# A fused group norm and attention kernel: TensorE keeps the kernel's own order, sums follow one burst later, and a batch's output projection runs beside the load two pairs further on

## The chip, the core and the metric

The kernel runs on one core of a Trainium2 chip. Five engines work side by side, each through its own queue of instructions: TensorE (PE, matrix products; its weight loads are shown as PEld), VectorE (DVE), ScalarE (ACT), GpSimd (POOL) and SyncE (SP). SP only issues DMA transfers here. The other engines can issue DMAs too, and DMA engines move the data. Instructions of different engines wait for each other through semaphores. [...]

The metric is the device time of one execution in microseconds (us), the median of several runs. The profile comes from one further execution, recorded by the hardware profiler.

## What is computed

The input x has 4 batches of 512 channels by 48 x 48 = 2304 positions. It is normalized in 32 groups of 16 channels, goes through attention with 8 heads of 64 channels, is projected, and is added to x again:

```python
hn = _group_norm(x, gn_scale, gn_bias)                # 32 groups, fp32
qkv = jnp.einsum('oc,bchw->bohw', qkv_w, hn) + qkv_b[None, :, None, None]
qkv = qkv.reshape(b, 3, num_heads, d, t).astype(jnp.float16)
q, k, v = (qkv[:, 0], qkv[:, 1], qkv[:, 2])
scale = jnp.asarray(1.0 / math.sqrt(math.sqrt(d)), dtype=jnp.float16)
w = jnp.einsum('bhct,bhcs->bhts', q * scale, k * scale)
w = jax.nn.softmax(w, axis=-1)
a = jnp.einsum('bhts,bhcs->bhct', w, v).astype(jnp.float32)
out = jnp.einsum('oc,bchw->bohw', proj_w, a.reshape(b, c, hh, ww)) + proj_b[None, :, None, None]
return x + out
```

## The kernel before

**Tiles and stages.** Channels lie on the 128 partitions, so a batch of x is four chunks of 128 x 2304. Two heads together fill 128 channels. The kernel therefore works on 16 pairs of heads in order, g = 4 x batch + pair. The queries of a pair are cut into five blocks (`QBLOCKS`): four of 512 and one of 256.

The work of a pair is cut into units. A unit covers 512 query columns in all: one key block of 128 keys for the blocks of 512 queries, two key blocks for the block of 256. That makes 4 x 18 + 9 = 81 units in a pair (`units_of`, L735). For a unit:

- `scores` (L743) computes keys times queries for both heads (L751) into a PSUM tile `ps` of 128 x 1024; there are two such tiles. One exp on ACT (L759) turns it into a tile `p` in fp16; there are six. No maximum is subtracted. DVE adds the p tiles of up to six units into a tile `acc` (L772).
- `values` (L774) multiplies v with p and sums over all keys of a block into a PSUM tile `av` (L787); there is one such tile. After six units a matmul with ones sums the columns of `acc` into the PSUM tile `sl` (L801).
- `finish` (L811), after the last keys of a block, copies `av` to `avx` (L815) and `sl` to `slx` (L817) on DVE, sends the sums through SP's DMAs and DRAM (`sums`, the reciprocal `inv`, `row`, then `ib`, the sums spread over the partitions), and multiplies `avx` by `ib` on POOL into the attention output `att` (L833).

Units go in bursts of two: the scores of a burst, then the values of the burst before, then `fill` (L883). The pair has an odd number of units, so in every second pair a burst holds the last unit of one block and the first of the next.

**Work beside the bursts.** What else PE must do is cut into items, kept in a list per pair (`beside`, filled by `put`, L843). Each item has a weight in us, and can have a place, a unit of the pair before which it isn't taken. `fill` takes items from the head of the list until their weights have caught up with the share of the pair's units that are done; an item whose place has not come stops the list. When the scores of pair g + 1 begin, what is left of pair g's list is run at once.

The items are:

- `qk_items(g)` (L614): q and k of pair g from the normalized x, in fp32. For each of five column blocks and four chunks of channels an item has two matmuls of 64 output rows (L629). After the fourth chunk DVE moves the result to fp16 with scale and bias (L638).
- `v_items(b)` (L663): v of a whole batch, 18 blocks of 128 positions by four chunks (L673), two matmuls of 64 output rows each; DVE adds the bias (L681).
- `proj_items(b, j)` (L693): the output projection for one query block. POOL casts `att` of four pairs to a tile `a32` (L700), of which there is one. Then come four row blocks m of eight matmuls each (L710: the projection weights are split into a high and a low part, `whi` and `wlo`), written as items of one channel chunk each. For each m SP loads a tile of x again, `res` (three buffers), DVE adds projection, bias and x (L719), and SP stores it.
- `turn` (L850): `load_x` for the next batch (L497, two DMAs for each chunk on POOL's queue, into the single buffers of x), then `norm` (L572): statistics on DVE (L577), means over groups by two small matmuls on PE (`gmean` L580, `gvar` L590), a power on POOL for 1/sqrt, and then four instructions of 128 x 2304 on DVE, one for each chunk, which apply the norm in place (L602).

All three kinds of items, and the small matmuls of the norm, use the same two PSUM tiles `pw`.

**Order.** The lists are filled in L848 to L869. For batches 0 to 2, pair 0 of a batch has q and k of pair 2 beside it, pair 1 those of pair 3, pair 2 has `turn` and the first 55 entries of the next batch's v, and pair 3 the rest of v, and q and k of the next batch's first pair (and of its second, but for batch 2). The projection of the batch before stands beside pairs 0 (four blocks) and 1 (one block). In the last batch each of the first three pairs has q and k of the next one; the last batch's own projection stands beside the last pair, each block's items not before 12 units after the block's end.

This is the order in which the instructions are written. [...] the built order of PE differs from the written one: in before the items' matmuls often stand between single units, and pieces of an item are apart.

**Start.** x of batch 0 is loaded over SP's and ACT's queues, the constants follow on SP's queue and the three parts of the q, k, v weights on ACT's. After the norm come q and k of pair 0, the splitting of the projection weights (`split_wproj`, L536: DMAs on SP, copies on DVE), v of batch 0, and q and k of pair 1. After the last burst the rest of the last projection runs as a tail, and a count over all sums sets a flag for a general path (`general_path`), which does not run with these inputs.

## Time and profile before

| what | us |
|---|---|
| median of 3 runs | 1922.71 (1918.26 to 1926.49) |
| profiled execution | 1919.6 |
| its span, first to last instruction | 1917.7 |

The busy time of each engine over the stretches of the profile that the first and last exp of a batch set (us; batch 0 holds pairs 0 to 3, and so on):

| stretch | length | PE | DVE | ACT | POOL |
|---|---|---|---|---|---|
| start, to the first exp | 160.1 | 127.6 | 49.1 | 1.3 | 3.1 |
| batch 0 | 446.1 | 426.2 | 268.4 | 315.0 | 31.7 |
| batch 1 | 453.5 | 441.0 | 281.7 | 314.2 | 45.2 |
| batch 2 | 427.5 | 412.7 | 276.7 | 314.2 | 44.4 |
| batch 3 | 402.4 | 393.6 | 256.5 | 314.5 | 46.0 |
| tail | 28.1 | 15.3 | 8.9 | 0.0 | 4.2 |

In the lines of a profile, L751 is line 751 of the kernel, "out<-in" names the tiles that an instruction writes and reads, then come partitions x elements of both, and "x4" how many instructions a line stands for. A bracket at the end of a line of the timeline names how long the engine stood idle before it, and what released it. "PEclk" and "clock" are the granted clock of PE as a share of full speed. [...]

### The profile page before, as it was taken

The page shows a single profiled execution, that of the slowest core. Times are in us where ns is not written, and L with a number is a line of the kernel's source. Part 1 is how long each engine was busy: PE and PEld are TensorE (multiplying, and loading weights), DVE is VectorE, ACT ScalarE, POOL GpSimd, SP SyncE. Part 2 cuts the span into 40 slices and gives each one's busy share as a digit, 9 for nine tenths or more (in the row PEclk, how much of TensorE's full clock was granted, in tenths as well). Part 3 has the DMA queues.
Part 4 walks back from the last instruction along what each step waited for, and adds up shares of the span by engine and source line. Part 5 has one row for each costly group of instructions (what it writes and reads, how often), then busy time and mean ns, then how long its engine had stood idle before and what let it go on. Part 6 is the DMA issues. An engine that isn't in the chain of part 4 may idle for free.

```text
span 1917.7 us, 27997 instructions
## 1 busy us (share of the span) xinstructions
PE 1816.3 (95%) x10644; PEld 656.0 (34%) x10644; DVE 1141.3 (60%) x1800; ACT 1259.2 (66%) x1297; POOL 174.7 (9%) x199
## 2 busy tenths in 40 slices
PE   3999999799999999989999999979999999999997
PEld 1333233223333353322333344332333344332334
DVE  5224566675555666685555566677566566665664
ACT  0005788685666768876665767877577767887872
POOL 0000000100000021110000011020000011000011
PEclk9999999899999999989999999989999999999998
DMA  5000000300000041310000032040000032010033
GB/s 203 1 1 1 12 15 18 108 12 12 9 7 14 23 144 34 121 34 12 9 12 7 15 99 90 13 143 12 12 9 12 15 107 82 18 46 12 15 100 104
DMA packets 88643, 82.20 MB, mean 43 GB/s; under 512 B 51636, under 2 KB 57780, under 8 KB 88500
## 3 DMA queue, kind: packets, MB, share of 16 engines
q1 hardware_dynamic: 82884, 60.67, 11.7%
q0 software_dynamic: 3456, 14.16, 2.0%
q10 hardware_dynamic: 2160, 5.51, 0.8%
q8 instruction: 85, 1.39, 0.3%
q14 instruction: 58, 0.48, 0.1%
HBM read 60.83 MB, written 19.17 MB: 42 GB/s over the span
## 4 chain that ended last, share of the span: by engine, by line
PE 78%; DMA 6%; ACT 5%; DVE 5%; issue 4%; POOL 1%; SPq 0%; ACTq 0%; DVEq 0%; POOLq 0%
PE pqk L629 26%; PE ps L751 16%; PE av L787 15%; PE pv L673 12%; PE pr L710 7%; ACT p L759 5%; PE sl L801 3%; DVE acc L772 3%; DMA x<-x_dram 2%; DMA out_dram<-x 1%; DMA sums<-slx 1%; DMA row<-inv 1%; DVE st L577 1%; DMA wqkv<-qkv_wT_dram 1%; DMA ib<-row 1%
## 5 line engine op out<-in xcount | busy, mean ns | idle before, releaser
L759 ACT ACTIVATE p<-ps 128x1024 f16<-128x1024 f32 x1296 | 1257.9, 1022 | 612.7 <-PE ps L751 583.5
L772 DVE TENSOR_TENSOR acc<-acc,p 128x1024 f16<-128x1024 f16 x848 | 617.3, 729 | 318.8 <-ACT p L759 305.8
L629 PE MATMUL pqk<-x,wqkv 128*64 128x512 f32 (+1 forms) x2560 | 621.4, 552 | 3.9 <-DVE x L602 3.9
L787 PE MATMUL av<-p,v 128*64 128x512 f16 (+1 forms) x2880 | 464.3, 374 | 2.2 <-DVE avx L815 2.2
L751 PE MATMUL ps<-q,k 64*128 64x512 f16 (+1 forms) x2880 | 448.1, 364 | 14.2 <-ACT p L759 7.1
L751 PEld LDWEIGHTS <-k 64*128 64x128 f16 x2880 | 120.7, 94 | 544.3 <-issue 534.4
L673 PE MATMUL pv<-wqkv,x 128*64 128x512 f32 x1152 | 278.3, 593 | 0.0
L629 PEld LDWEIGHTS pqk<-x,wqkv 128*64 128x64 f32 x2560 | 198.7, 137 | 190.1 <-issue 109.6
L772 DVE TENSOR_TENSOR acc<-p,p 128x1024 f16<-128x1024 f16 x224 | 157.2, 702 | 165.1 <-ACT p L759 163.9
L833 POOL TENSOR_TENSOR att<-avx,ib 128x512 f16<-128x512 f32 (+1 forms) x80 | 100.5, 1257 | 1537.0 <-DMA ib<-row 1302.1
L787 PEld LDWEIGHTS <-v 128*64 128x64 f16 x2880 | 128.9, 108 | 247.7 <-issue 241.8
L710 PE MATMUL pr<-a,whi 128*128 128x512 f32 (+1 forms) x320 | 131.5, 417 | 8.2 <-POOL a L700 6.1
L673 PEld LDWEIGHTS pv<-wqkv,x 128*64 128x64 f32 x1152 | 84.8, 137 | 114.6 <-issue 94.1
L710 PE MATMUL pr<-a,wlo 128*128 128x512 f32 (+1 forms) x320 | 121.5, 385 | 0.0
L801 PE MATMUL sl<-acc,ones 128*64 128x512 f16 (+1 forms) x512 | 95.7, 362 | 21.4 <-DVE acc L772 20.9
L681 DVE TENSOR_TENSOR v<-pv,bv 128x512 f16<-128x512 f32 x72 | 49.6, 689 | 71.5 <-PE pv L673 71.5
L815 DVE COPY avx<-av 128x512 f32<-128x512 f32 (+1 forms) x80 | 51.0, 637 | 55.6 <-PE av L787 55.5
L710 PEld LDWEIGHTS pr<-a,whi 128*128 128x128 f32 x320 | 61.4, 192 | 54.9 <-issue 24.6
L638 DVE TENSOR_SCALAR k<-pqk,bqk 128x512 f16<-128x512 f32 (+1 forms) x80 | 55.4, 692 | 35.2 <-PE pqk L629 34.7
L638 DVE TENSOR_SCALAR q<-pqk,bqk 128x512 f16<-128x512 f32 (+1 forms) x80 | 55.3, 691 | 35.3 <-PE pqk L629 34.3
L719 DVE SCALAR_TENSOR_TENSOR x<-pr,bproj,x 128x512 f32<-128x512 f32 (+1 forms) x80 | 55.3, 694 | 35.0 <-PE pr L710 22.6
L700 POOL CAST a<-att 128x512 fp32r<-128x512 f16 (+1 forms) x80 | 53.9, 705 | 143.7 <-PE pr L710 142.8
(41 smaller groups left out, 281.2 us busy)
## 6 DMA issues: line engine op xcount, KB each, us to landing
x<-x_dram SPq DMA_DIRECT2D x64, 256.0 KB, 2.9
ib<-row SPq DMA_DIRECT2D x128, 128.0 KB, 3.0
out_dram<-x SPq DMA_DIRECT2D x64, 256.0 KB, 3.0
x<-x_dram POOLq DMA_DIRECT2D x24, 576.0 KB, 7.2
wqkv<-qkv_wT_dram ACTq DMA_DIRECT2D x3, 1024.0 KB, 11.2
x<-x_dram SPq DMA_DIRECT2D x4, 576.0 KB, 7.7
x<-x_dram ACTq DMA_DIRECT2D x4, 576.0 KB, 9.6
sums<-slx SPq DMA_DIRECT2D x128, 2.0 KB, 2.0
```

The lines of the kernel that those rows point to most:

```text
L629: nc.tensor.matmul(pw[0][lo : lo + D, :n], wqkv[:, c, w0 + lo : w0 + lo + D], hn[b][c][:, o : o + n], start=(c == 0), stop=(c == NC - 1),)
L638: nc.vector.tensor_scalar(qk[g][part][:, o : o + n], pw[0][:, :n], SCALE, bqk[:, col : col + 1], ALU.mult, ALU.add,)
L673: nc.tensor.matmul(pw[0][lo : lo + D, :], hn[b][c][:, i * P + lo : i * P + lo + D], wqkv[:, c, 2 * C :], start=(c == 0), stop=(c == NC - 1),)
L700: nc.gpsimd.tensor_copy(at[0][:, c, :n], atts[b * NPAIR + c][:, o : o + n])
L710: nc.tensor.matmul(pw[0][:, :n], w[:, c, bass.ts(m, P)], at[0][:, c, :n], start=(c == 0 and i == 0), stop=(c == NC - 1 and i == 1),)
L719: nc.vector.scalar_tensor_tensor(xt, pw[0][:, :n], bproj[:, m : m + 1], xt, ALU.add, ALU.add)
L751: nc.tensor.matmul(ps[:, h, a * n : (a + 1) * n], k[rows, bass.ts(i, P)], q[rows, o : o + n], start=True, stop=True,)
L759: nc.scalar.activation(pt, ps, AF.Exp)
L772: nc.vector.tensor_tensor(acc[key], before, pt, ALU.add)
L787: nc.tensor.matmul(av[0][lo : lo + D, :n], vv[b][:, i, pr * P + lo : pr * P + lo + D], pt[:, h, a * n : (a + 1) * n], start=(i == 0), stop ...
L801: nc.tensor.matmul(sl[0][lo : lo + D, :n], ones16, t[:, h, a * n : (a + 1) * n], start=(m < SUMMED and a == 0), stop=(keys[-1] == NT - 1 a ...
L833: nc.gpsimd.tensor_tensor(atts[g][:, o : o + n], avx[:, :n], ib[:, :n], ALU.mult)
```

## The change

- The whole fast path is built under a manual order for PE: PE's instructions stand in the order in which the kernel writes them. The other engines are still arranged by the scheduler.
- The column sums (`sl`) of a burst's values are not run with them but put on a list, `late`, and run after the next burst's scores (`add_up`). The copy `avx` stands directly behind the last values of a block, and the rest of `finish` follows the late sums.
- The projection of batch b - 1 stands beside pair 2 of batch b, behind `turn`, in place of pairs 0 and 1. Its items are whole row blocks of eight matmuls with a weight of n / 290 us. As `att` lives longer, its pool has seven buffers in place of five.
- `norm` is cut in two. `norm_stats` runs with `turn`; `norm_apply` stands behind the projection in pair 2's list, not before unit 26, and applies the norm in blocks of columns: 20 instructions in place of 4.
- v of a batch is two half tiles, the first with one buffer and the second with two, in place of whole tiles with two; each evacuation is two instructions of 256 columns. Pair 2 has the first 41 entries of v, pair 3 the rest and q and k of both first pairs of the next batch, in all three batches. In the last batch q and k of its pairs 2 and 3 stand beside its pairs 0 and 1, as in the others.
- The last batch's projection blocks may start 14 units after their block's end, in place of 12.
- At the start the small constants are loaded over POOL's queue; of the weight parts k goes over SP's queue, q over ACT's, v over SP's. The written order is q and k of pair 0, v, q and k of pair 1; `split_wproj` stands at the head of pair 0's list, not before unit 10.

```diff
--- before.py
+++ after.py
@@ -482,8 +482,8 @@
     const = ctx.enter_context(tc.tile_pool(name="const", bufs=1))
     xpool = ctx.enter_context(tc.tile_pool(name="xpool", bufs=1))
     qkp = ctx.enter_context(tc.tile_pool(name="qkp", bufs=3))
-    vpool = ctx.enter_context(tc.tile_pool(name="vpool", bufs=2))
-    apool = ctx.enter_context(tc.tile_pool(name="apool", bufs=5))
+    vpool = ctx.enter_context(tc.tile_pool(name="vpool", bufs=1))
+    apool = ctx.enter_context(tc.tile_pool(name="apool", bufs=7))
     ppool = ctx.enter_context(tc.tile_pool(name="ppool", bufs=6))
     work = ctx.enter_context(tc.tile_pool(name="work", bufs=2))
     small = ctx.enter_context(tc.tile_pool(name="small", bufs=2))
@@ -511,18 +511,18 @@
-    nc.sync.dma_start(gsc, gn_scale)
+    nc.gpsimd.dma_start(gsc, gn_scale)
...
-    for part in (1, 0, 2):
+    for part, engine in ((1, nc.sync), (0, nc.scalar), (2, nc.sync)):
         cols = bass.ts(part, C)
-        nc.scalar.dma_start(
+        engine.dma_start(
             wqkv[:, :, cols], qkv_wT[:, cols].rearrange("(c p) o -> p c o", p=P)
         )
 
@@ -569,13 +569,19 @@
     sums = const.tile([P, NG, 2 * NT], F32, name="sums")
 
 
-    def norm(b):
+    mvs = {}
+
+    def norm_stats(b):
         mv = small.tile([P, NC, 2], F32, tag="mv", name=f"mv_{b}")
         for c in range(NC):
             st = small.tile([P, T // SB, 6], F32, tag="st", name=f"st_{b}_{c}")
             for j in range(T // SB):
                 nc.vector.bn_stats(st[:, j, :], hn[b][c][:, bass.ts(j, SB)])
             nc.vector.bn_aggr(mv[:, c, :], st.rearrange("p j s -> p (j s)"))
+        mvs[b] = mv
+
+    def norm_apply(b):
+        mv = mvs.pop(b)
         pm = ps_w.tile([P, NC], F32, tag="pw", name=f"gmean_{b}")
         nc.tensor.matmul(pm, gmat2, mv[:, :, 0], start=True, stop=True)
         mean = small.tile([P, NC], F32, tag="gmean", name=f"mean_{b}")
@@ -598,15 +604,12 @@
         nc.vector.tensor_tensor(mga, mean, ga, ALU.mult)
         gb = small.tile([P, NC], F32, tag="gb", name=f"gb_{b}")
         nc.vector.tensor_tensor(gb, gbi, mga, ALU.subtract)
-        for c in range(NC):
-            nc.vector.tensor_scalar(
-                hn[b][c],
-                hn[b][c],
-                ga[:, c : c + 1],
-                gb[:, c : c + 1],
-                ALU.mult,
-                ALU.add,
-            )
+        for o, n in QBLOCKS:
+            for c in range(NC):
+                t = hn[b][c][:, o : o + n]
+                nc.vector.tensor_scalar(
+                    t, t, ga[:, c : c + 1], gb[:, c : c + 1], ALU.mult, ALU.add
+                )
 
 
     qk = {}
@@ -664,7 +667,10 @@
         items = []
 
         def new():
-            vv[b] = vpool.tile([P, NT, C], F16, tag="v", name=f"v_{b}")
+            vv[b] = [
+                vpool.tile([P, NT, C // 2], F16, tag=f"v{i}", bufs=1 + i, name=f"v{i}_{b}")
+                for i in range(2)
+            ]
 
         def one(i, c, pw):
             if c == 0:
@@ -678,7 +684,11 @@
                     stop=(c == NC - 1),
                 )
             if c == NC - 1:
-                nc.vector.tensor_tensor(vv[b][:, i, :], pw[0], bv, ALU.add)
+                for half in range(2):
+                    cols = bass.ts(half, C // 2)
+                    nc.vector.tensor_tensor(
+                        vv[b][half][:, i, :], pw[0][:, cols], bv[:, cols], ALU.add
+                    )
 
         items.append((0.0, new))
         for i in range(NT):
@@ -701,36 +711,32 @@
                     at[0][:, c, :n], atts[b * NPAIR + c][:, o : o + n]
                 )
 
-        def one(m, c, pw):
...
+        def one(m):
+            ps = ps_w.tile([P, QB], F32, tag="pw", name=f"pr_{b}_{j}_{m}")
+            xt = work.tile([P, QB], F32, tag="res", bufs=3, name=f"x_{b}_{j}_{m}")[:, :n]
+            nc.sync.dma_start(xt, x[b, bass.ts(m, P), o : o + n])
+            for c in range(NC):
+                for i, w in enumerate((whi, wlo)):
+                    nc.tensor.matmul(
+                        ps[:, :n],
+                        w[:, c, bass.ts(m, P)],
+                        at[0][:, c, :n],
+                        start=(c == 0 and i == 0),
+                        stop=(c == NC - 1 and i == 1),
+                    )
+            nc.vector.scalar_tensor_tensor(
+                xt, ps[:, :n], bproj[:, m : m + 1], xt, ALU.add, ALU.add
+            )
+            nc.sync.dma_start(out[b, bass.ts(m, P), o : o + n], xt)
 
         items = [(0.0, load)]
         for m in range(NC):
-            pw = {}
-            for c in range(NC):
-                items.append((n / 1200.0, lambda m=m, c=c, pw=pw: one(m, c, pw)))
+            items.append((n / 290.0, lambda m=m: one(m)))
         return items
 
 
 
-    av, sl, pts, acc = {}, {}, {}, {}
+    av, sl, pts, acc, avx, late = {}, {}, {}, {}, {}, []
 
     def units_of(g):
         found = []
@@ -779,40 +785,45 @@
             if j == 0:
                 atts[g] = apool.tile([P, T], F16, tag="att", name=f"att_{g}")
             av[0] = ps_av.tile([P, QB], F32, tag="av", name=f"av_{g}_{j}")
-            sl[0] = ps_l.tile([P, QB], F32, tag="sl", name=f"sl_{g}_{j}")
         pt = pts.pop((g, j, keys[0]))
         for a, i in enumerate(keys):
             for h in range(2):
                 lo = h * D
                 nc.tensor.matmul(
                     av[0][lo : lo + D, :n],
-                    vv[b][:, i, pr * P + lo : pr * P + lo + D],
+                    vv[b][pr // 2][:, i, pr % 2 * P + lo : pr % 2 * P + lo + D],
                     pt[:, h, a * n : (a + 1) * n],
                     start=(i == 0),
                     stop=(i == NT - 1),
                 )
-        per = len(keys)
-        m = keys[0] // per
+        if keys[-1] == NT - 1:
+            avx[g, j] = work.tile([P, QB], F32, tag="avx", name=f"avx_{g}_{j}")
+            nc.vector.tensor_copy(avx[g, j][:, :n], av[0][:, :n])
+        m = keys[0] // len(keys)
         if m % SUMMED == SUMMED - 1 or keys[-1] == NT - 1:
...
+            late.append(lambda: add_up(g, j, m, len(keys), keys[-1] == NT - 1))
+
+    def add_up(g, j, m, per, last):
+        o, n = QBLOCKS[j]
+        if m < SUMMED:
+            sl[0] = ps_l.tile([P, QB], F32, tag="sl", name=f"sl_{g}_{j}")
+        t = acc.pop((g, j, m // SUMMED))
+        for a in range(per):
+            for h in range(2):
+                lo = h * D
+                nc.tensor.matmul(
+                    sl[0][lo : lo + D, :n],
+                    ones16,
+                    t[:, h, a * n : (a + 1) * n],
+                    start=(m < SUMMED and a == 0),
+                    stop=(last and a == per - 1),
+                )
+        if last:
             finish(g, j)
 
     def finish(g, j):
         o, n = QBLOCKS[j]
         per = n // P
-        avx = work.tile([P, QB], F32, tag="avx", name=f"avx_{g}_{j}")
-        nc.vector.tensor_copy(avx[:, :n], av[0][:, :n])
         slx = work.tile([P, QB], F32, tag="slx", bufs=1, name=f"slx_{g}_{j}")
         nc.vector.tensor_copy(slx[:, :n], sl[0][:, :n])
         first = 2 * o // P
@@ -831,7 +842,7 @@
                 ib[h * D : (h + 1) * D, :n], row[h : h + 1, :n].to_broadcast((D, n))
             )
         nc.gpsimd.tensor_tensor(
-            atts[g][:, o : o + n], avx[:, :n], ib[:, :n], ALU.mult
+            atts[g][:, o : o + n], avx.pop((g, j))[:, :n], ib[:, :n], ALU.mult
         )
 
 
@@ -845,35 +856,32 @@
 
     for b in range(B):
         g = b * NPAIR
+        put(g, qk_items(g + 2))
+        put(g + 1, qk_items(g + 3))
         if b + 1 < B:
 
             def turn(b=b):
                 hn[b + 1] = load_x(b + 1, (nc.gpsimd, nc.gpsimd))
-                norm(b + 1)
-
-            put(g, qk_items(g + 2))
-            put(g + 1, qk_items(g + 3))
-            vs = v_items(b + 1)
-            put(g + 2, [(0.0, turn), (45.0, lambda: None)] + vs[:55])
-            put(g + 3, vs[55:] + qk_items(g + 4))
-            if b + 2 < B:
-                put(g + 3, qk_items(g + 5))
-        else:
-            for pr in range(3):
-                put(g + pr, qk_items(g + pr + 1))
+                norm_stats(b + 1)
+
+            put(g + 2, [(0.0, turn)])
         if b > 0:
             for j in range(NQ):
-                put(g + j // 4, proj_items(b - 1, j))
+                put(g + 2, proj_items(b - 1, j))
+        if b + 1 < B:
+            put(g + 2, [(0.0, lambda b=b: norm_apply(b + 1))], 26)
+            vs = v_items(b + 1)
+            put(g + 2, vs[:41])
+            put(g + 3, vs[41:] + qk_items(g + 4) + qk_items(g + 5))
     ends = [i for i, u in enumerate(units_of(0)) if u[2][-1] == NT - 1]
     for j in range(NQ):
-        put(NG - 1, proj_items(B - 1, j), ends[j] + 12)
-
-    norm(0)
-    for _, run in qk_items(0):
+        put(NG - 1, proj_items(B - 1, j), ends[j] + 14)
+
+    norm_stats(0)
+    norm_apply(0)
+    for _, run in qk_items(0) + v_items(0) + qk_items(1):
         run()
-    split_wproj()
-    for _, run in v_items(0) + qk_items(1):
-        run()
+    beside[0].insert(0, (0.0, split_wproj, 10))
 
     stream = [u for g in range(NG) for u in units_of(g)]
     per_pair = len(stream) // NG
@@ -898,12 +906,16 @@
                 while beside[g - 1]:
                     beside[g - 1].pop(0)[1]()
             scores(u)
+        while late:
+            late.pop(0)()
         for u in waiting:
             values(u)
         waiting = burst
         fill(n + len(burst) - 1)
     for u in waiting:
         values(u)
+    while late:
+        late.pop(0)()
     for _, run, _ in beside[NG - 1]:
         run()
 
@@ -930,7 +942,8 @@
     nc = tc.nc
     keep = ctx.enter_context(tc.tile_pool(name="keep", bufs=1))
     flag = keep.tile([1, 1], I32, name="flag")
-    fast_path(tc, flag, *args)
+    with tc.manual_schedule(engines={mybir.EngineType.PE}):
+        fast_path(tc, flag, *args)
     fails = nc.values_load(
         flag[0:1, 0:1],
         min_val=0,
```

## The prediction

> **What bounds the kernel now.** I read the busy shares first, then the chain of waits, then the groups, and then the timeline of single stretches, because a share of busy time cannot say how well TensorE (PE) is filled.
>
> ```profile
> PE 1816.3 (95%) x10644; PEld 656.0 (34%) x10644; DVE 1141.3 (60%) x1800; ACT 1259.2 (66%) x1297; POOL 174.7 (9%) x199
> ...
> PE 78%; DMA 6%; ACT 5%; DVE 5%; issue 4%; POOL 1%; SPq 0%; ACTq 0%; DVEq 0%; POOLq 0%
> ...
> L759 ACT ACTIVATE p<-ps 128x1024 f16<-128x1024 f32 x1296 | 1257.9, 1022 | 612.7 <-PE ps L751 583.5
> ```
>
> PE is never long idle and carries 78% of the chain; ACT mostly waits for scores. So a gain must come from what PE does while it is "busy". A regular burst (two units of scores, two of values, two items of q/k projection) in the timeline:
>
> ```profile
> 611.93 0.60 PE L751 MATMUL ps<-q,k 64*128 64x512 f16 x4
> ...
> 612.47 0.62 PE L787 MATMUL av<-p,v 128*64 128x512 f16 x4
> ...
> 612.92 1.88 PE L629 MATMUL pqk<-x,wqkv 128*64 128x512 f32 x8
> ...
> 614.74 0.61 PE L751 MATMUL ps<-q,k 64*128 64x512 f16 x4
> ```
>
> By starts: scores 0.54, values 0.45, two items 1.82 (0.10 + 0.86 each, an item being two matmuls of 64 output rows that run side by side); 2.81 in all. An earlier stretch looks otherwise:
>
> ```profile
> 335.17 1.02 PE L629 MATMUL pqk<-x,wqkv 128*64 128x512 f32 x2
> ...
> 336.12 0.39 PE L751 MATMUL ps<-q,k 64*128 64x512 f16 x2
> ...
> 336.44 0.41 PE L787 MATMUL av<-p,v 128*64 128x512 f16 x2
> ...
> 336.68 1.02 PE L629 MATMUL pqk<-x,wqkv 128*64 128x512 f32 x2
> ```
>
> Here the scheduler has put half an item between units: half the array runs alone, and 1.51 us go by per unit. The built order has 148 such odd stretches of fp32 matmuls. Third, the turn to the next batch:
>
> ```profile
> 365.43 0.41 PE L787 MATMUL av<-p,v 128*64 128x512 f16 x2
> ...
> 372.33 0.56 DVE L577 BATCH_NORM_STATS2 st<-x 128x6 f32<-128x384 f32 x1 [3.89 <-DMA x<-x_dram]
> ...
> 376.05 3.86 ACT L759 ACTIVATE p<-ps 128x1024 f16<-128x1024 f32 x4 [10.98 <-DVE acc L772]
> ...
> 376.23 0.59 PE L580 MATMUL gmean<-mv,gmat 128*128 128x4 f32 x2 [10.39 <-DVE mv L578]
> ```
>
> The statistics wait on VectorE (DVE) for the last chunk of x, the acc adds stand behind them, the p buffers run out, and ACT and PE stop for 10 us. The windows table then shows the granted clock at 0.50 from 370 to 382.
>
> [...] idle from 365.8, halved within 368 to 370, full again within 382 to 384, some 6.7 us after work resumed. [...] matmuls on different tiles of the array overlap, which is the pair of halves above (0.86 us for two, 0.86 for one). [...] in this trace the acc adds indeed stand behind a statistics instruction that waits for a DMA.
>
> **The parts.** I count by pairs of heads (81 exps each, counted in the trace). The first exp starts at 160.1, the last ends at 1889.6, the rest is a tail of 28.1. The sixteen pairs took 102.1, 94.6, 120.7, 128.6; 115.8, 91.5, 117.6, 128.6; 115.8, 91.8, 118.5, 101.4; 115.8, 90.2, 99.8, 96.6: 1729.5.
>
> *PE's own work* is not changed. A pair's attention is 40.5 bursts x 0.99 + 15 sums x 0.22 + some 38 starts of items x 0.10 = 47. q and k of a pair are 36 full items, 31.0; v of a batch 72 items, 61.9; a projection 16 x 2.16 + 4 x 1.15 = 39 (eight matmuls start 0.23 apart; a burst with eight lasts 3.15). Pair 4 of before (q/k and four projection blocks) makes 47 + 31 + 35 = 113 against 115.8, and pair 3 (90 items) 124 against 128.6: pairs full of work lose little. The loss is in pairs 0, 1, 5, 9, 13, 14 (7 to 24 each over content) and at the turns.
>
> *PE in the kernel's order* removes every odd stretch (the built order of after has none). But with one item to a burst, PE (1.95) and ACT (1.94) are coupled through two score buffers: from 1650.54 to 1663.29 six unsplit bursts took 12.75, so 2.125 each. Pairs with q/k alone: 34 x 2.125 + 6.5 x 1.9 = 84.7. Those are now 0, 1, 4, 5, 8, 9, 12, 13.
>
> *New waits for avx.* One PSUM buffer holds av. A pair has 81 units, so in odd pairs a burst holds a block's last values and the next block's first, and PE stands between them until DVE has copied av. Before shows the wait where values follow so directly:
>
> ```profile
> 1260.46 0.41 PE L787 MATMUL av<-p,v 128*64 128x256 f16 x4 [1.00 <-DVE avx L815]
> ```
>
> Five per odd pair; behind the waiting values stand items and the next scores. With ACT's slack off (0.25 in bursts without items, 0.9 with one, 1.0 with more): 3.7 in pairs 1, 5, 9, 13 and 5 in 3, 7, 11. Low end: DVE is free at once, 0.7 each; high: it is in an acc add, 1.5. I take 0.9. So the eight light pairs: 8 x 84.7 + 4 x 3.7 + 3 (the first starts with four bursts empty) = 695.
>
> *Pairs 3, 7, 11* get 32 items of v and 72 of q/k: 47 + 104 x 0.86 + 5 = 141.5 each, 424.
>
> *Turns.* DVE's built order again has all statistics of chunks 1 to 3 ahead of the second acc add, and POOL's again has one att multiply ahead of the last half chunk's DMA, in all three batches. From first issue (347.85) to the last statistics (375.4) that chain took 27.5; nothing removed shortens it. The new order issues the load some 6 us before the pair starts (9 before), since the last q item comes later. In pairs 6 and 10, two projections run, then the third finds both work buffers full, since DVE evacuates the first behind the statistics: PE stops 16 after the first issue and goes on at some 28: 12 idle, 1.5 of small waits, half clock for 6.7 (3.4 lost). Then a32 has one buffer: each next block's four POOL casts (1.17 for two) begin when the last projection ends, 2.4 less the 1.0 of attention between, over four blocks 5. The norm: gmean stands behind the last projection, and its DVE reader behind that one's evacuation (2), the small steps and gvar 1.5, rstd, ga, gb and the first block 3.0 (1.05 to 1.42 on POOL alone), clock 1.5: 8. The applying by blocks saves 0.7 of 1.4 per chunk there. Content 47 + 40 x 0.86 + 39 = 120.6; with 30.4, 151 each. Pair 2 has no projection: 13 empty bursts x 1.87 (six exps in 5.61) = 24.3, stall 14, clock 3.4, one burst with norm and 15 items at once 1 + 5 + 13 + 1, then 26 x 2.125 = 55: 117. Together 419. High end: the chain is longer than in before, since the residual's DMAs run beside it, +8 each; low end: the stall gone, -15 each.
>
> *Pairs 14 and 15.* Projection in every second burst, 3.15 and then some 2 because the scores of the next burst wait for ACT: 101. The last pair has three blocks of four at once (8.6 each, of which ACT has 1 as cover, and 2 of wait for att, a burst later than before): 75.7 + 3 x 9.7 = 105. The tail: two blocks, eight residual tiles through three buffers, out and in again some 6.6: 28 as before.
>
> *Start.* The small loads go to POOL's queue, v's weights to SP's; SP then issues wproj some 6 earlier. whi and wlo still stand between the steps of the norm on DVE. Applied by blocks, PE starts after a 512-wide step in place of 1476 ns: I take -3 (nothing to -5). Split v evacuation: 72 more DVE instructions of some 0.15 us net, DVE at 60%: nothing, and 11 us if DVE were full.
>
> Sum: 157 + 695 + 424 + 419 + 206 + 28 = 1929 of span, against 1917.7. The measured median before is 1922.71, 1.0026 of the span; so 1929 x 1.0026 = 1934, +0.6%. PE's fill is repaired, but the work is heaped in pairs 3, 6, 7, 10, 11, the light pairs are bound by the coupling (some 7 each), and PE, which may not step over a wait, pays for each.
>
> **Rivals.** A: the projection covers the load. For it: before had only values and scores to run there. It decides if the last statistics come within 16 us of the first issue, or if one more evacuation passes ahead of them: 3 x 15.4 less, 1883 x 1.0026 = 1888. Against it: DVE's order. B: the residual binds. Between row and ib, SP waits for a DMA (146 us in 75 waits), and out and x stand behind it. Three tiles go round in 3.0 + 2.9 + 0.75 + 0.8 = 7.5, in 3 x 3.15 of PE; with 5 us of blocking each round it is 12.5, +1.0 x 20 tiles x 2 batches = 40: 1974. C: the order isn't what binds and nothing changes, 1922; the built order speaks against it.
>
> **Numbers.** Forecast 0.50 (its own range 1915 to 1955; half a per cent, about what can be told from no change, is 1913 to 1932: of its chance 0.05 below, 0.17 between, 0.28 above), A 0.28 (0.27 faster, 0.01 same), B 0.17, C 0.05. Faster 0.32, same 0.23, slower 0.45. Range 1888 to 1976.
>
> **What would show it.** Right: no lone fp32 half in the timeline; av waiting 1.0 for avx some 40 times; pairs 4, 8, 12 near 85 and 3, 7, 11 near 141; 12 us of idle PE and half a clock after each load, ended by pr or sl waiting for DVE; waits of pr for a's casts. Wrong: pairs 6 and 10 under 135 (A), or over 165 with pr waiting for x's DMA (B); light pairs at 80 would mean that scores and exp don't couple in order.

## The result

The changed kernel took 1940.9 us (median of 4 runs, 1938.9 to 1943.9) against 1922.5 before: a ratio of 1.0097, 95% interval 1.0072 to 1.0123. It is slower by about 1%. The forecast was 1934 in a range of 1888 to 1976, with the chance of "slower" at 0.45.

From the page of the kernel after, first the busy shares, then the chain that ended last by engine, then three of the groups (busy time, mean ns of one, idle time before them and what ended most of it):

```profile
PE 1727.2 (89%) x10644; PEld 640.8 (33%) x10644; DVE 1173.6 (61%) x1936; ACT 1246.2 (64%) x1297; POOL 174.2 (9%) x204
...
PE 69%; ACT 9%; DMA 7%; DVE 6%; issue 6%; POOL 2%; SPq 0%; ACTq 0%; DVEq 0%; POOLq 0%
...
L765 ACT ACTIVATE p<-ps 128x1024 f16<-128x1024 f32 x1296 | 1244.9, 1028 | 654.7 <-PE ps L757 639.6
...
L757 PE MATMUL ps<-q,k 64*128 64x512 f16 (+1 forms) x2880 | 436.7, 362 | 74.0 <-ACT p L765 64.3
...
L792 PE MATMUL av<-p,v 128*64 128x512 f16 (+1 forms) x2880 | 409.6, 368 | 35.2 <-DVE avx L801 34.6
```

The two PE groups in the page of before:

```profile
L787 PE MATMUL av<-p,v 128*64 128x512 f16 (+1 forms) x2880 | 464.3, 374 | 2.2 <-DVE avx L815 2.2
L751 PE MATMUL ps<-q,k 64*128 64x512 f16 (+1 forms) x2880 | 448.1, 364 | 14.2 <-ACT p L759 7.1
```

PE is busy 89 us less than before for the same 10644 matmuls, and yet the span is 22 us longer. The work is packed more tightly, and PE waits more: the scores now wait 64 us for exps (7 before), the values 35 us for `avx` (2 before). The chain shows the same: PE's share fell from 78 to 69%, and ACT, DVE, DMA and issue took it.

By pairs of heads (us, from the first exp of one to the first exp of the next; where several pairs are named, their mean):

| stretch | before | forecast | after |
|---|---|---|---|
| start | 160.1 | 157 | 159.9 |
| pair 0 | 102.1 | 88 | 88.7 |
| pairs 1, 5, 9, 13 | 92.0 | 88.4 | 89.3 |
| pairs 4, 8, 12 | 115.8 | 84.7 | 86.0 |
| pair 2 | 120.7 | 117 | 118.5 |
| pairs 3, 7, 11 | 119.6 | 141.5 | 142.3 |
| pairs 6, 10 | 118.1 | 151 | 145.7 |
| pairs 14, 15 | 196.4 | 206 | 207.1 |
| tail | 28.2 | 28 | 32.0 |
| span | 1917.7 | 1929 | 1939.6 |

Much of this is work that was moved: the projection left pairs 4, 8, 12 for 6, 10, 14, and pair 11, which took 101.4 before, now has q and k of pair 13 and more of v. The time that the light pairs gave up came back in the heavy pairs 3, 7, 11 and in the turns 6 and 10. That is the picture of the forecast. Its causes still had to be tried, since a sum can come out right with wrong terms.

### The profile page after: what moved, and what is told of

The parts are those of the page before. It is cut to its first block, busy times and chain, and to the rows that moved or that the text cites. A ratio compares the mean times of both kernels' runs of the same rounds, so it can differ in the third digit from the quotient of the medians.

```text
span 1939.6 us, 28173 instructions
## 1 busy us (share of the span) xinstructions
PE 1727.2 (89%) x10644; PEld 640.8 (33%) x10644; DVE 1173.6 (61%) x1936; ACT 1246.2 (64%) x1297; POOL 174.2 (9%) x204
## 4 chain that ended last, share of the span: by engine, by line
PE 69%; ACT 9%; DMA 7%; DVE 6%; issue 6%; POOL 2%; SPq 0%; ACTq 0%; DVEq 0%; POOLq 0%
PE pqk L632 22%; PE ps L757 14%; PE av L792 12%; PE pv L679 12%; ACT p L765 9%; PE pr L720 6%; PE sl L814 3%; DVE x L610 2%; DVE acc L778 2%; DMA x<-x_dram 2%; DMA sums<-slx 1%; DVE avx L801 1%; DMA row<-inv 1%; DMA ib<-row 1%; POOL a L710 1%
## 5 line engine op out<-in xcount | busy, mean ns | idle before, releaser
L765 ACT ACTIVATE p<-ps 128x1024 f16<-128x1024 f32 x1296 | 1244.9, 1028 | 654.7 <-PE ps L757 639.6
L778 DVE TENSOR_TENSOR acc<-acc,p 128x1024 f16<-128x1024 f16 x848 | 610.3, 720 | 239.8 <-ACT p L765 218.1
L632 PE MATMUL pqk<-x,wqkv 128*64 128x512 f32 (+1 forms) x2560 | 559.2, 551 | 3.1 <-DVE x L610 2.9
L757 PE MATMUL ps<-q,k 64*128 64x512 f16 (+1 forms) x2880 | 436.7, 362 | 74.0 <-ACT p L765 64.3
L792 PE MATMUL av<-p,v 128*64 128x512 f16 (+1 forms) x2880 | 409.6, 368 | 35.2 <-DVE avx L801 34.6
L757 PEld LDWEIGHTS <-k 64*128 64x128 f16 x2880 | 124.3, 94 | 579.2 <-issue 567.2
L679 PE MATMUL pv<-wqkv,x 128*64 128x512 f32 x1152 | 269.2, 599 | 9.2 <-DVE x L610 8.7
L778 DVE TENSOR_TENSOR acc<-p,p 128x1024 f16<-128x1024 f16 x224 | 163.8, 731 | 172.2 <-ACT p L765 171.1
L632 PEld LDWEIGHTS pqk<-x,wqkv 128*64 128x64 f32 x2560 | 181.2, 137 | 183.3 <-issue 107.4
L689 DVE TENSOR_TENSOR v<-pv,bv 128x256 f16<-128x256 f32 x144 | 54.6, 418 | 60.7 <-PE pv L679 60.5
L727 DVE SCALAR_TENSOR_TENSOR x<-pr,bproj,x 128x512 f32<-128x512 f32 (+1 forms) x80 | 55.7, 696 | 45.9 <-PE pr L720 27.6
L828 DVE COPY slx<-sl 128x512 f32<-128x512 f32 (+1 forms) x80 | 50.8, 635 | 27.5 <-PE sl L814 25.3
## 6 DMA issues: line engine op xcount, KB each, us to landing
x<-x_dram SPq DMA_DIRECT2D x4, 576.0 KB, 10.9
```

Of the source, the lines that this page charges most:

```text
L632: nc.tensor.matmul(pw[0][lo : lo + D, :n], wqkv[:, c, w0 + lo : w0 + lo + D], hn[b][c][:, o : o + n], start=(c == 0), stop=(c == NC - 1),)
L679: nc.tensor.matmul(pw[0][lo : lo + D, :], hn[b][c][:, i * P + lo : i * P + lo + D], wqkv[:, c, 2 * C :], start=(c == 0), stop=(c == NC - 1),)
L727: nc.vector.scalar_tensor_tensor(xt, ps[:, :n], bproj[:, m : m + 1], xt, ALU.add, ALU.add)
L757: nc.tensor.matmul(ps[:, h, a * n : (a + 1) * n], k[rows, bass.ts(i, P)], q[rows, o : o + n], start=True, stop=True,)
L765: nc.scalar.activation(pt, ps, AF.Exp)
L778: nc.vector.tensor_tensor(acc[key], before, pt, ALU.add)
```

## The experiments

All twelve were run beside the kernel before, so each ratio is to that kernel. Pair times are from the profile of each. An experiment on an experiment names its base.

### The order of PE, taken away and given alone

e1 is the changed kernel without the manual order; e2 is the kernel before with it.

```diff
-    with tc.manual_schedule(engines={mybir.EngineType.PE}):
-        fast_path(tc, flag, *args)
+    fast_path(tc, flag, *args)
```

> The changed kernel, but PE's instructions are arranged by the scheduler again; everything else of the change stays. My theory, that the manual order is what closes the odd stretches of fp32 matmuls (lone halves of the array), says: the light pairs with q/k alone (0, 1, 4, 5, 8, 9, 12, 13; 86 to 89 us in the changed kernel) go up to what such pairs had before, 91 to 95, and the heavy pairs 3, 7, 11 from 142 to about 146; at the turns PE may step over a wait again, so pairs 6 and 10 may lose up to 10. In all +20 to +60 us on the changed kernel: 1960 to 2000. Rival (the order of PE is not what matters, the placing of the work is): within 8 us of 1941, light pairs unchanged.

> The kernel before, with the manual order for PE alone added. My theory says two effects of opposite sign: light pairs 1, 5, 9 fall from 91 to 95 to about 86 to 89 and pair 0 from 102 to about 89 (in all some -30), and the three turns grow, because gmean stands in PE's order right behind the load: from 118 to 121 to 135 to 145 each (+50 to +75). Sum +20 to +45: about 1945 to 1965, slower than before. Rival (the manual order is a gain by itself): under 1915, with the turns near 120.

e1: 1951.0 us, ratio 1.0150 (1.0132 to 1.0167). e2: 1940.0 us, 1.0103 (1.0084 to 1.0122). PE's rows in the timeline of e1, pair 4:

```profile
631.25 0.39 PE L757 MATMUL ps<-q,k 64*128 64x512 f16 x2
...
631.82 1.02 PE L632 MATMUL pqk<-x,wqkv 128*64 128x512 f32 x2
632.77 0.39 PE L757 MATMUL ps<-q,k 64*128 64x512 f16 x2
```

and of the kernel after, also pair 4:

```profile
628.34 0.65 PE L757 MATMUL ps<-q,k 64*128 64x512 f16 x4
...
629.37 1.02 PE L632 MATMUL pqk<-x,wqkv 128*64 128x512 f32 x4
630.33 0.82 PE L757 MATMUL ps<-q,k 64*128 64x512 f16 x4
```

In e1 half an item (x2) costs the same 1.02 us as a whole one (x4), and 1.52 us go by for one unit; after needs 1.99 for two units and a whole item. So the lone halves are back without the order, and the light pairs show it: 93.8 in place of 86.0 (4, 8, 12) and 97.5 in place of 88.7 (pair 0). But the turns are shorter without it, 111.4 (118.5) and 139.0 (145.7), as are pairs 14 and 15, 196.6 (207.1). Only some 10 us of the median are left as the order's gain, half of the least I expected (20 to 60); the heavy pairs, 141.6, did not rise at all.

e2 shows the other side. The order alone makes pair 0 14.6 us shorter, and pair 2 14.6 longer, since PE now stands at the norm's first matmul. Its wait in the timeline of e2:

```profile
358.72 0.59 PE L580 MATMUL gmean<-mv,gmat 128*128 128x4 f32 x2 [18.56 <-DVE mv L578]
```

Before it waited 10.4 us there. The sum, 18 us, is a little under the 20 that I expected at least. Pairs 6 and 10 grew to 124.3 and 125.2 only, not to 135. My guess for the light pairs was wrong in part: 5 and 9 rose from 91.7 to 96.2. In the trace PE waits there 4.5 and 4.9 us for `avx` (1.0 each before), and over the whole kernel 27.3 us in 39 waits, where before had 2.2. So the fixed order alone brings the wait for `avx` too. That an order by hand is a gain by itself is refuted for this kernel: it trades lone halves for waits that PE may no longer step over.

### The sums one burst later

```diff
-        while late:
-            late.pop(0)()
         for u in waiting:
             values(u)
+        while late:
+            late.pop(0)()
```

> The changed kernel, but the column sums run directly behind the values of their own burst again, not behind the next burst's scores. My theory: the late place matters only where the acc adds are late on DVE, that is around the loads and in the light pairs a little, so +5 to +15 (1945 to 1956), and PE's waits of sl for acc rise from 18 us to 30 or more. Rival (the sums' place is worth nothing): 1938 to 1944. If sums in place are faster, under 1938, the late place is itself a cost.

1972.8 us, ratio 1.0258 (1.0228 to 1.0289): 32 us slower than after, twice what I expected at most. The waits of the two kernels, e5 and then after (us in total, times, longest):

```profile
PE sl L814 <- DVE acc L778: 44.8, 31, 14.6
```

```profile
PE sl L814 <- DVE acc L778: 17.9, 6, 10.9
```

The rise of 26.9 us is most of the 30.5 in the span. In the light pair 4, where no load runs, five such waits, 2.1 us together, are about the growth, 86.0 to 88.2. In the heavy pairs nothing changed. So with PE's order fixed, the late place of the sums is worth more than any other single part that was tried alone, and the prediction had no term for it.

### The wait for avx in odd pairs

e4 ends the bursts with the pair, so that no burst holds two blocks.

```diff
-    for n in range(0, len(stream), 2):
-        burst = stream[n : n + 2]
+    starts = [
+        n for n in range(len(stream)) if n % per_pair % 2 == 0
+    ]
+    for n in starts:
+        burst = stream[n : min(n + 2, n - n % per_pair + per_pair)]
```

> The changed kernel, but bursts end with the pair: the last of a pair's 81 units is a burst of its own, so no burst holds the last unit of one block and the first of the next. My theory (in every second pair the values of a new block wait for the copy avx inside a burst, 0.7 to 0.9 us five times) says: pairs 1, 5, 9, 13 go from 89.3 to about 86, pairs 3, 7, 11 from 142.3 to about 138, PE's waits for avx from 35 us to under 5; in all -20 to -28, about 1917. Rival (the 3.3 us more in odd pairs have another cause, or the burst of one unit costs as much): 1935 or above.

1904.4 us, ratio 0.9909 (0.9890 to 0.9928): faster than both kernels. The wait in the timeline of after, pair 13, on PE and on DVE:

```profile
1632.82 0.41 PE L792 MATMUL av<-p,v 128*64 128x512 f16 x2
1634.08 0.41 PE L792 MATMUL av<-p,v 128*64 128x512 f16 x2 [0.86 <-DVE avx L801]
```

```profile
1633.34 0.69 DVE L801 COPY avx<-av 128x512 f32<-128x512 f32 x1 [1.07 <-PE av L792]
```

The last values of a block end at 1633.23, the copy follows at once and takes 0.69, and the next block's values start 0.86 after the last ones ended. The trace of e4 has no wait of PE for `avx`. Pair 13 fell from 89.3 to 85.7 and pairs 3, 7, 11 from 142.3 to 137.0, as expected. The total fell by 36.5 us, more than the 20 to 28 expected: pair 2 fell by 3.3 and pairs 6 and 10 by 5.9 each, which I had not forecast and whose cause was not tried. Pairs 1, 5, 9 did not fall (89.6), which was not expected either; the timeline of e4 at the end of pair 5 shows why:

```profile
755.86 1.14 SPq L832 DMA_DIRECT2D sums<-slx  x2
755.89 2.72 POOL L503 DMA_DIRECT2D x<-x_dram  x5 [9.30 <-PE pqk L632]
...
763.64 0.20 DVE L834 RECIPROCAL inv<-sums 128x8 f32<-128x8 f32 x1 [5.52 <-DMA sums<-slx]
763.77 0.67 DVE L778 TENSOR_TENSOR acc<-acc,p 128x1024 f16<-128x1024 f16 x1
...
764.49 0.64 PE L814 MATMUL sl<-acc,ones 128*64 128x256 f16 x4 [4.66 <-DVE acc L778]
```

The sums go out together with the load of x. Of their two transfers the second lands 7.2 us after its issue in place of the usual 2.0, the reciprocal waits for it at the head of DVE's queue, the acc add behind it is late, and PE stands at the sum.

### What the load holds up

e8 (on e4) moves the reciprocal to POOL, as a power of -1.

```diff
...
-        nc.vector.reciprocal(inv[:, :, :per], sm)
+        nc.gpsimd.tensor_tensor(inv[:, :, :per], sm, mone[:, :, :per], ALU.pow)
```

> The kernel of e4, with the reciprocal of the sums (inv) on POOL in place of DVE, as a power of -1. In e4 pair 5, PE stopped 4.7 us because a sum waited for an acc add that stood on DVE behind inv, which waited 5.5 us for the sums' DMA under the load of x. If DVE's waits for these small DMAs are what makes pairs 1, 5, 9 (88.7, 91.1, 89.2) longer than 13 (85.7), they fall to 86 to 87, the turns by 1 to 3 each: 1888 to 1898. Rival (the acc adds then wait for something else, or POOL's queue delays att and x): 1900 or above.

1919.3 us, ratio 0.9987 (0.9978 to 0.9996), 15 us slower than e4. Pairs 1, 5, 9 fell to 85.7 each, as pair 13: the cause above is shown. The rival came true all the same, that POOL's queue then delays `att` and x: pair 2 rose from 115.2 to 118.9, and pairs 6 and 10 from 139.8 to 147.9. In pair 6 POOL waits 6.7 us for the sums and 9.2 for `ib` ahead of the last two half chunks of x, issues these only at 779.1, and PE stands 9.4 us for an evacuation that has the statistics ahead of it on DVE (4.6 in e4).

e3 (on after) issues the statistics chunk by chunk over the first 20 units, kept in that order on DVE; e6 (on e3) also moves the casts of `att` from POOL to DVE.

```diff
                 hn[b + 1] = load_x(b + 1, (nc.gpsimd, nc.gpsimd))
-                norm_stats(b + 1)
...
+                if n in at:
+                    put(g + 2, [chunk[at[n]]], (5, 9, 13, 19)[at[n]])
+                put(g + 2, proj[n : n + 1])
```

```diff
-                nc.gpsimd.tensor_copy(
+                nc.vector.tensor_copy(
                     at[0][:, c, :n], atts[b * NPAIR + c][:, o : o + n]
                 )
```

> The changed kernel, but the statistics of the next batch are issued chunk by chunk, spread over the first 20 units of the turning pair and kept in that order on DVE, in place of all at once with the load. My theory (the statistics that wait for x hold up the acc adds and the evacuations behind them on DVE, so p and pw run out and PE stops and is clocked down) says that the stall of 12 us and the half clock go: pair 2 from 118 to about 101, pairs 6 and 10 from 145 to about 131, in all -40 to -50: about 1895, faster than both kernels. Rival (the turn is bound by the norm's own chain and the casts of the single a32 buffer, and the stall is only moved): -10 or less, 1930 or above.

> The kernel of e3 (statistics spread), and the casts of att to a32 run on DVE in place of POOL. In e3 the second block's casts stood on POOL behind an att multiply that waited for ib, and pr waited 8.5 us for them. If that is the wait which took the place of the statistics, then pairs 6 and 10 fall from 144 to 131 to 134 and the time from 1931 to about 1908. Rival (the load's traffic slows every small DMA, and the next waiting instruction on DVE or SP holds PE instead): pairs 6 and 10 stay above 140, gain under 6 us.

e3: 1931.0 us, ratio 1.0048 (1.0031 to 1.0064), 10 us better than after, not 40 to 50. e6: 1930.0 us, 1.0045 (1.0035 to 1.0055), nothing more. My theory of the turn fell; the rival, that the stall is only moved, was right. In after, the stall of pair 6 had looked as predicted:

```profile
787.34 0.59 POOL L503 DMA_DIRECT2D x<-x_dram  x1
...
791.30 1.48 DVE L579 BATCH_NORM_STATS2 st<-x 128x6 f32<-128x384 f32 x3 [2.00 <-DMA x<-x_dram]
792.69 0.73 DVE L727 SCALAR_TENSOR_TENSOR x<-pr,bproj,x 128x512 f32<-128x512 f32 x1
...
793.48 0.79 PE L720 MATMUL pr<-a,whi 128*128 128x512 f32 x1 [7.01 <-DVE x L727]
```

The evacuation L727, for which PE stands, has the statistics ahead of it, and these wait for the last half chunk of x. In e3 the statistics are gone from that place, and in POOL's and PE's rows one reads:

```profile
782.77 1.11 POOL L503 DMA_DIRECT2D x<-x_dram  x2
785.22 1.22 POOL L713 CAST a<-att 128x512 fp32r<-128x512 f16 x2 [1.34 <-PE pr L723]
794.73 0.72 POOL L847 TENSOR_TENSOR att<-avx,ib 128x256 f16<-128x256 f32 x1 [8.29 <-DMA ib<-row]
795.40 1.16 POOL L713 CAST a<-att 128x512 fp32r<-128x512 f16 x2
```

```profile
796.05 0.80 PE L723 MATMUL pr<-a,whi 128*128 128x512 f32 x1 [8.53 <-POOL a L713]
```

PE waits 8.5 us at nearly the same point, now because half of the casts for the next projection block stand on POOL behind an `att` that waits for `ib`. In e6, with the casts on DVE, three waits of 3.1, 2.4 and 3.4 us stood before `pr` in their place.

### The norm in steps, the load paced, the waits unblocked

e7 (on e4) moves q and k of a batch's second pair from the heavy pair to the pair after it.

```diff
+        if b > 0:
+            put(g, qk_items(g + 1))
         put(g, qk_items(g + 2))
...
-            put(g + 3, vs[41:] + qk_items(g + 4) + qk_items(g + 5))
+            put(g + 3, vs[41:] + qk_items(g + 4))
```

> The kernel of e4 (bursts end with the pair), and q and k of a batch's second pair move from the heavy pair before the batch to its first pair, so that pairs 4, 8, 12 have 72 items and pairs 3, 7, 11 have 68. My theory of the coupling (a burst with one item costs 2.125 where PE has 1.95 of work, a burst with two costs its own 2.81) says: pairs 3, 7, 11 fall from 137 to 105 to 108, pairs 4, 8, 12 rise from 85.7 to 110 to 112, together -4 to -7 a batch, about 1889. Rival (PE's work is simply moved; no coupling is lost): within 3 us of e4, 1901 to 1907.

1892.5 us, ratio 0.9839 (0.9813 to 0.9865). Pairs 3, 7, 11 fell from 137.0 to 108.1 and pairs 4, 8, 12 rose from 85.7 to 110.6: 4.0 us won in each batch, by no more than spreading the same items, at the low end of the 4 to 7 expected. That fits the coupling: a burst with one item is bound by scores and exps that wait for each other, a burst with two by PE's own work. ACT alone does not set the light pairs: in pair 4 of e4 it is busy for 77.9 of 85.7 us.

e9 (on e7) cuts the norm's steps into three bursts; e10 (on e9) issues the eight transfers of x one in a burst from ACT's queue, with the statistics spread as in e3.

```diff
...
+            for at in (26, 28, 30):
+                put(g + 2, [(2.0, step)], at)
```

```diff
...
+                i = nc.scalar.dma_start(
+                    hn[b + 1][c][:, cols], x[b + 1, bass.ts(c, P), cols]
+                )
+                tc.keep_in_program_order(i)
...
```

> The kernel of e7, with the applying of the norm cut into three steps (up to the variance; gvar to the coefficients; the blocks) that are taken in three different bursts, not before units 26, 28 and 30. In e7 pair 6 PE stands 2.7 us before gvar and 2.5 before the first v item[...]. If these waits are real cost and not hidden by another, pairs 2, 6 and 10 fall by 6 to 8 each (116 to 109, 139 and 142 to 132 to 135), 1892 to about 1871. Rival (the bursts without items that the steps need are paid later, since PE's work is only pushed back): under 3 us each, 1884 or above.

> The kernel of e9, with the load of the next batch's x cut into its eight transfers, one for each burst, issued from ACT's queue behind the exps in place of POOL's all at once; the statistics follow chunk by chunk as in e3, and projection items stand between. My theory (the load at once fills the DMA engines, the transfers of the sums take 7 in place of 2 us, and what waits for them on DVE and POOL stops PE for 5 to 12 us and halves its clock) says that the stall at the start of pairs 2, 6, 10 goes: pair 2 to 100 to 104, pairs 6 and 10 to 120 to 125, total about 1835 to 1850. Rival (the issue on ACT holds up the exps, or the casts of a single a32 bind the turn anyway): pairs 6 and 10 stay at 130 or above, 1860 or more.

e9: 1898.5 us, ratio 0.9891 (0.9874 to 0.9907), 6 us more than e7, where I had expected some 20 less: the waits at `gvar` shrank (in pair 6 from 2.7 to 0.6), but the scheduler put sixteen applying instructions in a row on DVE, 7.9 us, and a sum waited 7.9 us for the acc add behind them. e10: 1881.2 us, ratio 0.9798 (0.9782 to 0.9815). Pairs 1, 5, 9 fell to 85.9, which agrees with the load as what had held them, though the statistics moved in the same edit. Pairs 6 and 10 stayed at 142.2 (140.5 in e7), where the rival had put them, and not at 120 to 125. Two waits are left there in e10: `pr` for the casts behind an `att` (7.5 and 8.4 us) and `av` for an `avx` behind nineteen applying instructions (6.8 and 7.2).

e12 (on e10) acts on both, with `att` on POOL five bursts later and one block of the norm to a burst, and keeps the start free as in e11:

```diff
...
+        if g < NG - 1:
+            held.append([5, multiply])
+        else:
+            multiply()
...
+            yield
             for c in range(NC):
                 t = hn[b][c][:, o : o + n]
```

> The kernel of e10 with three more edits, each against a wait that its trace shows: the att multiply is queued on POOL five bursts later (in e10 the casts for the next projection block stood behind an att that waited 7 us for ib, and PE waited 7.5 to 8.4 us for the casts in pairs 6 and 10); the norm is applied one block to a burst (in e10 nineteen applying instructions in a row held DVE 8.2 us, and PE waited 6.8 and 7.2 us for avx behind them); and the start is kept free of the weights' splitting as in e11 (-6.4 there). My theory (a turn is a chain of such waits, and what is left after these is PE's own work, 120 us in pairs 6 and 10) says pairs 6 and 10 fall from 141 and 143 to 122 to 128, pair 2 from 113 to 104 to 108, the start to 153.5: total about 1835 to 1845. Rival (another wait takes each one's place again, as in e3 and e9): pairs 6 and 10 at 135 or above, total 1860 or more.

1870.7 us, ratio 0.9720 (0.9704 to 0.9736), the fastest of all. The start came to 154.0 as expected, but pair 2 only to 110.6 (104 to 108 expected) and pairs 6 and 10 only to 140.6, and the rival is right once more. The timeline of e12, pair 6:

```profile
770.03 0.37 ACTq L895 DMA_DIRECT2D x<-x_dram  x1
...
770.51 1.94 ACT L776 ACTIVATE p<-ps 128x1024 f16<-128x1024 f32 x2 [4.93 <-DMA out_dram<-x]
...
774.57 0.75 DVE L738 SCALAR_TENSOR_TENSOR x<-pr,bproj,x 128x512 f32<-128x512 f32 x1 [5.28 <-DMA x<-x_dram]
```

Now exps stand on ACT's queue behind a transfer of x that was issued at 770.03, and on DVE the projection's evacuation waits 5.3 us for the residual. An acc add stands behind it, and PE waits 3.1 us for that. What would make a turn as short as PE's own work stays open.

### The projection's place and the start

e11 (on after) puts the projection back beside the first two pairs, and pins `split_wproj` on DVE behind what is written ahead of it.

```diff
-                put(g + 2, proj_items(b - 1, j))
+                put(g + j // 4, proj_items(b - 1, j))
...
-            nc.vector.tensor_copy(whi[:, c, :], w)
+            tc.keep_in_program_order(nc.vector.tensor_copy(whi[:, c, :], w))
```

> The changed kernel, with the projection of a batch back beside the first pair (four blocks) and the second (one block) of the next batch, as in the kernel before; and the splitting of the projection weights is kept from going ahead of the norm of batch 0 on DVE. Projection: my theory (PE's content is only moved, and beside the load part of it covers the stall) says pairs 4, 8 rise from 86 to 115 to 118, pairs 5, 9 from 89 to 93 to 97, pairs 6, 10 fall from 145 and 146 to 115 to 119 as pair 2: +2 to +12 for both batches. Rival A, stated with the prediction (the projection covers the whole load): +25 or more. If the projection beside the load costs more than it covers: -5 or less. Start: the first exp comes at 154 to 156 in place of 159.9, since DVE's copy of the mean waited 4.6 us behind the weights; if the q/k/v weights or the norm's chain bind the start, no change.

1943.3 us, ratio 1.0123 (1.0106 to 1.0140). The three pairs 4 to 6, 8 to 10 and 12 to 14 took 322.0, 324.5 and 284.3 in place of 320.4, 321.6 and 280.0: its place two pairs further on is worth 8.8 us in three batches, 4.5 of them in the two where a load runs beside it. As expected, pairs 4 and 8 took 117.3; pairs 6 and 10, 109.4 and 109.1, were shorter than I thought (115 to 119). The projection does not hide the load (that would have been 25 or more), and its new place does not cost. The start fell to 153.5. DVE in after, and in e11:

```profile
21.60 0.32 DVE L580 BATCH_NORM_AGGREGATE mv<-st 128x2 f32<-128x36 f32 x1
26.52 0.43 DVE L540 CAST whi<-wproj 128x512 fp32r<-128x512 f32 x1 [4.60 <-DMA wproj<-proj_wT_dram]
...
28.65 0.15 DVE L588 COPY mean<-gmean 128x4 f32<-128x4 f32 x1
```

```profile
21.84 0.32 DVE L580 BATCH_NORM_AGGREGATE mv<-st 128x2 f32<-128x36 f32 x1
22.91 0.16 DVE L588 COPY mean<-gmean 128x4 f32<-128x4 f32 x1 [0.74 <-PE gmean L586]
```

In after the statistics end 4 us earlier than in before (21.9 against 26.1), and all of it is lost, because the copy of the mean stands on DVE behind the splitting of the weights, which waits for their transfer.

## Why the prediction was right, and where not

The direction, the size (0.6% forecast, 0.97% measured) and the pattern over the pairs came out. In the span the forecast was 10.6 us short. By its own terms, rounded: start +2.9, light pairs +8.9, heavy pairs +2.9, turns -9.1, pairs 14 and 15 +1.1, tail +4.0. That the sum came so near is in part luck: all terms but one were too small, and the turns, too large, hid half of it.

- **PE in the kernel's order removes every odd stretch, and the light pairs come to 85 to 88.** Right, shown by e1: in the trace of after no stretch of fp32 matmuls ends in half an item. That waits would replace part of it is shown by e1 and e2.
- **Coupling of PE and ACT through two score buffers, 84.7 a pair.** Right in kind: 85.7 where no block straddles and no load runs (e4, e8), and e7 wins 4.0 a batch by avoiding it. The term was 0.9 to 1.3 a pair too small, and over eight pairs that is nearly all of the 8.9. (Its own sum, 34 x 2.125 + 6.5 x 1.9, is 84.6.)
- **New waits for `avx`, 0.9 each, five to an odd pair.** Right: 0.8 on average, 43 times, and gone in e4.
- **Pairs full of work lose little.** Right: 142.3 for 141.5.
- **Turns: the statistics stall PE for 12 us, and half a clock follows.** Right in kind, too large in size. PE's longest wait was 10.9 us in pair 2, 7.0 in pair 6 and 9.5 in pair 10. In pairs 6 and 10 PE stopped 18.4 and 16.2 us after the first transfer of the load was issued (forecast 16) and went on 25.4 and 25.7 after it (forecast 28). The casts into the single `a32`, put at 5 us a turn, appear in PE's waits with 0.5 and 0.8. (The terms of these two pairs add up to 150.3, not 151.) The granted clock fell within the 7.0 us: in pair 6 of after PEclk is 1.00 from 788 to 790, 0.80 from 790 to 792, 0.50 from 792 to 798 and 1.00 from 798 to 804. The matmuls `pr` start 0.43 us apart from 794.07 to 796.63, and 0.23 apart from 799.02 on.
- **The low end, "the stall gone, -15 each", and rival A.** Both counted the stall alone, and did not come. Rival A needed the last statistics early, or one more evacuation ahead of them. e3 gives the second: the statistics no longer stand ahead of the evacuation. But pair 2 won only 4 us and pairs 6 and 10 won 1.9 each, not 15.4, because other waits took the place of the first: the casts behind an `att` that waits for `ib` in e3, an evacuation that waits for the residual in e12. Small transfers do land late beside the load (up to 7.3 us for the sums in after). Yet with the load paced, in e10 (up to 5.0), the two pairs were no shorter, so how much of a turn the load itself causes stays open.
- **Rival B, the residual binds.** Not in after, where the evacuations on DVE wait for it 13.4 us in all. In e12 they wait 25.6, once other waits are out of the way.
- **Start, -3.** Wrong: it came to -0.2. The prediction named the steps of `whi` and `wlo` between those of the norm but gave them no price; e11 shows 6.4 us.
- **Tail, as before.** It grew by 3.8 us. The last full block's `att` begins 3.0 us after the last exp in before and 5.6 in after. The late sums are not the cause, since e5 without them has 5.1 and a tail of 32.1. The order is not the cause alone: the tail is 29.2 in e1, without it, but 28.4 in e2, with it. What the cause is stays open.
- **The late sums** were listed as a part and given no term. They are worth 32 us (e5). Since the pairs were summed from bursts that hold no wait for a sum, the forecast had silently taken them as free, which with the late place they nearly are.

## What to carry to other kernels

An engine in the order of the program is only as good as the waits that this order meets. If you fix the order, look in the same edit for consumers that can stand one step behind their producer: here the late sums were worth 32 us, and bursts that end with the pair 36. Where a burst of transfers ran, removing the one wait that the profile named bought little or nothing in the turns (e3, e6, e8, e9, e12), because a wait in another queue came next; look at the head of each queue at that moment, not at one. Light and heavy stretches of the same kernel can have different limits, so moving the same work from one to the other can pay by itself: e7 won 12 us with three lines.

## What the runs showed of the hardware

- A 2 KB transfer of the sums, issued from SP, landed in 2.0 us in after (median of 128). The two that were issued from 769.41 on, while the load of x ran (eight transfers of 576 KB; the DMA share is 0.90 to 1.06 in each 2 us from 770 to 780), took 6.4 and 7.3.
- Half an item of fp32 matmuls, on half the array, took as long as a whole one: 1.02 us for x2 (e1, at 631.82) and for x4 (after, at 629.37).
- Matmuls overlap in the records, so busy time of PE does not tell how well the array is used: the 2560 of q and k in after have a mean of 551 ns, 1411 us in all, and PE is busy for 559.2 us with them.
- An instruction that waited held up what stood behind it in its engine's queue: in pair 6 of after the statistics on DVE waited 2.00 us for x, the evacuation behind them began at 792.69, and PE, waiting for it, stood 7.01 us.
- With x issued from ACT's queue in place of POOL's, exps stood behind the issue: 4.9 us in e12, pair 6. The trace does not show what the issue itself waited for.
